# The first context tile in four chunks on a second queue, and the four denominator products issued together, in a cross-attention and mixture-of-experts kernel

## The chip, the cores and the metric

The kernel runs on one core of a Trainium2 chip. A core has a matrix engine (TensorE, PE in the profile, with its weight loads in a row of their own, PEld), a vector engine (VectorE, DVE), an activation engine (ScalarE, ACT), a general engine (GpSimd, POOL) and a sync engine (SyncE, SP) that issues most of the transfers. Each engine runs its own instructions in order and waits on semaphores for the others. The metric is the device time of the one core in microseconds. Three runs of the kernel before took 637.48, 638.38 and 639.96 us; their median is 638.38 us.

## The reference

The inputs are a batch of four sequences x of 512 tokens, width 512, and a context of 1,024 rows for each. The computation is one block of cross-attention and one feed-forward layer with eight experts, each behind a layer norm and added to x. The attention is the linear kind, in 16 heads of width 32:

```python
q = feature_map(norm(x) @ Wq.T)             # feature_map: x > 0 ? x + 1 : exp(x)
gate = sigmoid(norm(x) @ Wg.T + bg)
k, v = split(ctx @ Wkv.T)                   # feature_map on k
kv_summary = einsum('bhsd,bhse->bhde', k, v)
z = 1.0 / (einsum('bhld,bhd->bhl', q, k.sum(-2))[..., None] + EPS)
attn = einsum('bhld,bhde->bhle', q, kv_summary) * z
x = x + (attn * gate) @ Wo.T
```

Then every token of the new x goes to the two experts (of eight) with the largest logits, and their outputs are added with softmax weights.

## The kernel before

Everything is float32. A product is one `matmul` call of at most 128 x 128 weights against 512 columns; in the trace each such call stands as two matmul records[...].

**Setup.** SP issues all input transfers in the order of the program (`load`, L92). The first is `ctx_tiles[0, 0] = load_ctx(0, 0)` (L118): one 256 KB transfer of the first 128 context rows, already transposed in memory, so that each partition gets one row of 2,048 B, which holds four chunks `c` of 128 columns. Then come the four chunks of the key half of `wkv` (L121, 256 KB each), the second context tile, the four chunks of the value half, and the rest. The first matmul of the program, `pk` for tile (0, 0), multiplies chunk 0 of the context tile with chunk 0 of `wkv`, and so needs the first two transfers; the next needs the next chunk of `wkv`, and so on.

**Context.** For each batch `kv_tiles` (L281) goes over eight tiles of 128 context rows. A tile takes four products for its keys (`pk`), the feature map on DVE and ACT (L200 to L202), four products for its values (`pv`), which ACT copies out of PSUM (L258), and four small products that add the tile before to the sums (`kvs`).

**Queries.** For each batch the main loop (L692) makes `pq` (16 products), `pg` for the gates (16, with a sigmoid on ACT that writes `aT`, L325), the denominators `pd` (4 products with 32 output columns each) and their inverse `z` on DVE (L340, L341). Then it calls `products` (L344, called at L720).

**Products.** `z` holds one row for each head. `pz[g]` spreads these rows over the 128 partitions of group `g` by a product with a constant 0/1 matrix: 32 rows of the array, all 128 columns, at row offset `32 * g`. `pn[g]` are the numerators: for each group four products of 32 rows and 32 columns, each in its own place of the array. DVE multiplies `aT` by `pz` (L373) and by `pn` (L374). The groups go in two pairs, and PE gets its instructions in the order of the program (`keep_in_program_order`, L86): two `pz`, eight `pn`, two `pz`, eight `pn`.

What follows depends on the batch. For batches 0 to 2, the first half of the next batch's context tiles comes next (L723), so that PE goes on with `pk` and `pv` of the next batch's tile 0. For batch 3 it is the first four tiles of the experts' work (L725): each takes four transposes (`pt`), a copy on ACT, and four products (`pe`). Only after that does `attention_out` (L727) use `aT`.

**Buffers.** All these PSUM tiles come from one pool of six buffers (`pmm`, tag `mm`, L76), used in turn: a product may start when the reader of the tile that is six places ahead in this order is done.

**The second half** routes tokens to experts. Rows are scattered to a stream in device memory by indirect transfers, read back as tiles of 128 rows, multiplied with the expert's weights (`pe`, 35 tiles), scattered to `result`, and read back and added to `x` at the end.

Of the kernel before, what the change touches and what calls it, by code (L numbers as in the profile page):

```python
# [9 lines left out]
F32 = mybir.dt.float32  # L10
# [3 lines left out]
ALU = mybir.AluOpType  # L14
# [3 lines left out]
P = 128  # L18
B, L, S, D = 4, 512, 1024, 512
E, F = 8, 512  # L20
HD = 32
NC = D // P
NT = L // P
NS = S // P
# [7 lines left out]
ROW = D + 2  # L32
# [16 lines left out]
def xattn_moe_kernel(  # L49
# [14 lines left out]
    nc = tc.nc  # L64
# [6 lines left out]
    cpool = ctx.enter_context(tc.tile_pool(name="ctx", bufs=3))  # L71
# [4 lines left out]
    pmm = ctx.enter_context(tc.tile_pool(name="pmm", bufs=6, space=PSUM))  # L76
# [8 lines left out]
    def matmul(**operands):  # L85
        tc.keep_in_program_order(nc.tensor.matmul(**operands))  # L86
# [5 lines left out]
    def load(dst, src):  # L92
        tc.keep_in_program_order(nc.sync.dma_start(out=dst, in_=src))

    def load_ctx(b, s):
        t = cpool.tile([P, ROW], F32, tag="cT", name=f"cT_{b}_{s}")
        t = t[:, 0:D].rearrange("p (c n) -> p c n", n=P)
        load(t, cT[b, s])
        return t
# [15 lines left out]
    we_sb = wpool.tile([P, E, NC, F], F32, name="we_sb")  # L115

    ctx_tiles = {}
    ctx_tiles[0, 0] = load_ctx(0, 0)  # L118
    for half in range(2):
        for c in range(NC):  # L120
            load(wkv_sb[:, c, ts(half, D)], wkv[:, c, ts(half, D)])  # L121
        if half == 0:
            ctx_tiles[0, 1] = load_ctx(0, 1)
# [35 lines left out]
    spread = const.tile([P, NC, HD], F32, name="spread")  # L159
    nc.gpsimd.memset(spread, 1.0)  # L160
    for g in range(NC):
        r = slice(g * HD, (g + 1) * HD)
        for i in range(NC):
            o = (i + g) % NC
            nc.gpsimd.affine_select(
                out=spread[r, o, :], in_=spread[r, o, :], pattern=[[0, HD]],
# [8 lines left out]
        out=before, in_=before, pattern=[[1, P]], compare_op=ALU.is_gt, fill=0.0,  # L175
# [21 lines left out]
    def feature_map(dst, src):  # L197

        ex = work.tile([P, D], F32, tag="ex", name="ex")
        nc.vector.tensor_scalar(ex, src, 0.0, None, ALU.min)  # L200
        nc.scalar.activation(ex, ex, AF.Exp)  # L201
        nc.vector.scalar_tensor_tensor(dst, src, 0.0, ex, ALU.max, ALU.add)  # L202
# [34 lines left out]
    def half_tile(ct, half, name):  # L237
        ps = pmm.tile([P, D], F32, tag="mm", name=name)
        for c in range(NC):
            matmul(  # L240
                out=ps,
                lhsT=ct[:, c, :],
                rhs=wkv_sb[:, c, ts(half, D)],
                start=(c == 0),
                stop=(c == NC - 1),
            )
        return ps

    def keys(b, s):
        k = kvpool.tile([P, D], F32, tag="k", name=f"k_{b}_{s}")  # L250
        feature_map(k, half_tile(ctx_tiles[b, s], 0, "pk"))
        return k

    def values(b, s):
        pv = half_tile(ctx_tiles.pop((b, s)), 1, "pv")
        v = kvpool.tile([P, NC, P + 1], F32, tag="v", name=f"v_{b}_{s}", bufs=2)
        nc.gpsimd.memset(v[:, :, P : P + 1], 1.0)  # L257
        nc.scalar.copy(v[:, :, 0:P], pv.rearrange("p (g f) -> p g f", f=P))  # L258
        return v

    def kv_add(psum, s, k, v):

        for g in range(NC):
            matmul(
                out=psum[:, g, 0 : P + 1],
                lhsT=k[:, ts(g, P)],
                rhs=v[:, g, :],
                start=(s == 0 and g % 2 == 0),
                stop=(s == NS - 1),
                skip_group_check=True,  # L270
            )
# [6 lines left out]

    sums, pending, made = {}, {}, {}

    def kv_tiles(b, lo, hi, between=None):  # L281
        for s in range(lo, hi):
            nxt = (b, s + 2) if s + 2 < NS else (b + 1, s + 2 - NS)
            if nxt[0] < B and nxt != (0, 2):
                ctx_tiles[nxt] = load_ctx(*nxt)
            if b in (1, 2) and s % 2 == 0:
                e = (b - 1) * E // 2 + s // 2
                load(we_sb[:, e], we[e])
            if (b, s) == (3, 0):
                load(stream[SLOTS : SLOTS + P, :], empty)  # L290
            if s == 0:
                sums[b] = pkv.tile([P, NC, 2 * P], F32, tag="kvs", name="kvs")
            k = made.pop(s) if s in made else keys(b, s)
            if (b, s) == (0, 0):
                made[1] = keys(0, 1)
            v = values(b, s)
            if s > 0:
                kv_add(sums[b], s - 1, *pending[b])
            pending[b] = k, v
            if between is not None:  # L300
                between(s - lo)
        if hi == NS:
            kv_add(sums[b], NS - 1, *pending[b])
# [14 lines left out]
    def query(g, xT):  # L318
        qT = work.tile([P, L], F32, tag="qT", name="qT", bufs=NC)
        feature_map(qT, project(wq_sb, g, xT, "pq"))  # L320
        return qT
# [21 lines left out]

    def products(qTs, z, aT):  # L344

        for groups in ((0, 1), (2, 3)):
            pz = {g: pmm.tile([P, L], F32, tag="mm", name="pz") for g in groups}
            pn = {g: pmm.tile([P, L], F32, tag="mm", name="pn") for g in groups}
            for g in groups:
                r = slice(g * HD, (g + 1) * HD)  # L350
                matmul(
                    out=pz[g],
                    lhsT=spread[r].rearrange("p o e -> p (o e)"),
                    rhs=z[r, :],
                    start=True,
                    stop=True,
                    tile_position=(g * HD, 0),
                )

            for i in range(NC):  # L360
                for g in groups:
                    r = slice(i * HD, (i + 1) * HD)
                    o = (i + g) % NC * HD
                    matmul(
                        out=pn[g][o : o + HD, :],
                        lhsT=h_kv[r, g, :],
                        rhs=qTs[g][r, :],
                        start=True,
                        stop=True,
                        tile_position=(i * HD, o),  # L370
                    )
            for g in groups:
                nc.vector.tensor_tensor(aT[:, g, :], pz[g], aT[:, g, :], ALU.mult)  # L373
                nc.vector.tensor_tensor(aT[:, g, :], pn[g], aT[:, g, :], ALU.mult)  # L374

    def attention_out(b, aT):
        for t in range(NT):
# [148 lines left out]
    def per_expert(name):  # L526
        return const.tile([P, E], F32, name=name)
# [164 lines left out]
    for b in range(B):  # L692
        more = b + 1 < B
        qTs = [query(g, xT) for g in range(2)]
        if b > 0:
            dispatch(b - 1)
        qTs += [query(g, xT) for g in range(2, NC)]
        aT = big.tile([P, NC, L], F32, tag="aT", name="aT")
        gate(0, xT, aT)
        z = inverses(qTs)  # L700
        for g in range(1, NC):
            gate(g, xT, aT)
        if not more:
            whole = per_expert("whole")
            nc.vector.tensor_scalar(whole, counts[b - 1], float(1 - P), None, ALU.add)
            full = tiles_of(whole, "full")
            held = [tiles_of(counts[1], "held2"), tiles_of(counts[2], "held3")]
            none = per_expert("none")
            nc.vector.memset(none, 0.0)
            ahead = per_expert("ahead")  # L710
            nc.vector.tensor_tensor(ahead, held[0], full, ALU.min)
            early_groups = spans([none, ahead, full], "A")
            early_list = listed(early_groups, EARLY, "A")
            be_sb = wpool.tile([P, E, F], F32, tag="wkv", name="be_sb")
            load(
                be_sb.rearrange("p e f -> p (e f)"),
                be.rearrange("(o e) f -> o (e f)", o=1).to_broadcast([P, E * F]),
            )
            early = run(early_list, 0, EARLY, True)
        products(qTs, z, aT)  # L720
        if more:
            xs[b + 1] = load_x(b + 1)
            kv_tiles(b + 1, 0, NS // 2)  # L723
        else:
            for _ in range(4):  # L725
                next(early)
        attention_out(b, aT)  # L727
        choice = choose(b, *layernorm_stats(xs[b]))
        if more:
            ln = layernorm_stats(xs[b + 1])  # L730
            xT = new_xT()

            def between(i):
                normalized_T(xT, i, xs[b + 1], *ln)
                next(choice)

            kv_tiles(b + 1, NS // 2, NS, between)
            next(choice)
            kv_blocks(sums[b + 1])
# [14 lines left out]
    _, many, upto = early_groups  # L754
# [59 lines left out]
    first, last = 2 * NT, (B - 1) * NT  # L814
# [76 lines left out]
```

## Time and profile before

The profiled execution took 640.01 us, of which the span from first to last instruction is 638.3 us; 1.7 us lie around it.

| engine | busy us | share of the span |
|---|---|---|
| PE (matmul) | 606.4 | 95% |
| PEld (weight load) | 301.6 | 47% |
| DVE | 236.1 | 37% |
| ACT | 135.5 | 21% |
| POOL | 109.0 | 17% |

The parts of the kernel that the change touches, from the page and the timeline:

| what | count | busy us | mean ns of one record |
|---|---|---|---|
| `pk` products | 256 records | 118.6 | 608 |
| `pg` products | 128 records | 56.7 | 595 |
| gate times `pz` on DVE, one | 16 | | 681 (median) |
| `pz` products | 32 records | | 640 (median) |
| `pn` products | 128 records | | 600 (median) |
| wait of PE before the first `pk` | 1 | 4.6 (idle) | |

A matmul record's own duration is not what it costs: matmuls are pipelined, and the next starts before the one before has ended. The cost of a step on PE is the distance between starts, which the timeline shows. In a line of the timeline the first number is the start in us from the span's start, the second the time until the group's last end, and `x8` the number of records in the group; the bracket gives the idle time before it and what ended that.

### The profile page before, as it was taken

Reading aid. Unit: us, or ns where it says so; the run is one execution under the profiler, and the core shown is the slowest. Engines: PE = TensorE matmul, PEld = TensorE weight load, DVE = VectorE, ACT = ScalarE, POOL = GpSimd, SP = SyncE. Lnnn points to the kernel's source line nnn. Section 1 sums busy time; section 2 is a strip of 40 time slices with the busy share of each in tenths; the row PEclk is TensorE's granted clock in tenths of the full one; section 3 lists DMA queues with packets and bytes.
Section 4 is the critical chain, followed back from the end, with each engine's and each line's share of the span. In section 5 each row is a group of like instructions: output and inputs, shape, how many; then the busy total and the mean of one; then the engine's idle time right before and its main releaser. Section 6 shows DMA issues by size and latency. Waiting matters only on the chain. (4 is left out here: it accounts for less than half of the span.)

```text
span 638.3 us, 6238 instructions
## 1 busy us (share of the span) xinstructions
PE 606.4 (95%) x2044; PEld 301.6 (47%) x2044; DVE 236.1 (37%) x562; ACT 135.5 (21%) x215; POOL 109.0 (17%) x244
## 2 busy tenths in 40 slices
PE   7999999999999999999999999999999999999950
PEld 3555543544564345455543544654444654444420
DVE  2222243126224521632534135148424272111583
ACT  1322222113322122042221113322111221111100
POOL 3100000000004000000230000005241354643420
PEclk9999999999999999999999999999999999999985
DMA  8611400220253023022130100033430269647768
GB/s 301 194 34 37 144 0 2 104 93 17 82 166 115 18 62 111 26 91 93 47 117 17 34 16 16 1 131 134 116 116 33 84 203 264 193 133 258 278 236 300
DMA packets 27376, 70.50 MB, mean 110 GB/s; under 512 B 4240, under 2 KB 4240, under 8 KB 25936
## 3 DMA queue, kind: packets, MB, share of 16 engines
q1 hardware_dynamic: 19680, 48.31, 23.7%
q0 software_dynamic: 5360, 17.60, 7.6%
q10 hardware_dynamic: 2304, 4.20, 1.8%
q8 instruction: 17, 0.28, 0.2%
q14 instruction: 15, 0.12, 0.1%
HBM read 45.93 MB, written 24.16 MB: 110 GB/s over the span
## 5 line engine op out<-in xcount | busy, mean ns | idle before, releaser
L86 PE MATMUL pe<-we_sb,xgT 128*128 x280 | 125.9, 594 | 1.1 <-issue 0.6
L86 PE MATMUL pk<-wkv_sb,cT 128*128 128x512 f32 x256 | 118.6, 608 | 4.6 <-DMA wkv_sb<-in_wkv_dram 4.6
L86 PE MATMUL pv<-wkv_sb,cT 128*128 128x512 f32 x256 | 114.9, 592 | 0.0
L86 PEld LDWEIGHTS pv<-wkv_sb,cT 128*128 128x128 f32 x256 | 48.6, 190 | 61.2 <-issue 61.0
L200 DVE TENSOR_SCALAR ex<-pk 128x512 f32<-128x512 f32 x32 | 22.0, 689 | 148.0 <-PE pk L86 148.0
L86 PEld LDWEIGHTS pe<-we_sb,xgT 128*128 128x128 f32 x280 | 50.6, 190 | 53.0 <-issue 52.0
L86 PEld LDWEIGHTS pk<-wkv_sb,cT 128*128 128x128 f32 x256 | 47.7, 194 | 58.1 <-issue 54.3
L257 POOL MEMSET v<- 128x4 f32 x32 | 3.3, 106 | 347.1 <-PE kvs L86 284.1
L201 ACT ACTIVATE ex<-ex 128x512 f32<-128x512 f32 x48 | 30.2, 630 | 138.7 <-DVE ex L200 128.8
L86 PE MATMUL pg<-xT,wg_sb 128*128 128x512 f32 x128 | 56.7, 595 | 0.0
L86 PE MATMUL pq<-xT,wq_sb 128*128 128x512 f32 x128 | 56.6, 596 | 0.0
L659 DVE TENSOR_TENSOR y<-pe,be_sb 128x512 f32<-128x512 f32 x35 | 24.1, 690 | 87.4 <-PE pe L86 73.5
L86 PE MATMUL po<-wo_sb,aT 128*128 128x512 f32 x128 | 55.6, 592 | 0.0
L225 ACT COPY xgT<-pt 128x512 f32<-128x512 f32 x35 | 20.3, 587 | 121.9 <-PE pt L89 103.5
L670 POOL DMA_INDIRECT result<-y,to x35 | 37.5, 1071 | 39.0 <-DVE y L659 32.1
L505 POOL DMA_INDIRECT stream<-row,slot x32 | 32.1, 1003 | 49.6 <-DVE cmp L533 22.5
L86 PEld LDWEIGHTS kvs<-v,k 128*128 128x128 f32 x256 | 33.3, 191 | 13.4 <-issue 13.4
L86 PEld LDWEIGHTS pg<-xT,wg_sb 128*128 128x128 f32 x128 | 24.0, 190 | 32.1 <-issue 32.1
L86 PEld LDWEIGHTS po<-wo_sb,aT 128*128 128x128 f32 x128 | 24.1, 190 | 29.2 <-issue 28.9
L86 PEld LDWEIGHTS pq<-xT,wq_sb 128*128 128x128 f32 x128 | 23.8, 190 | 27.3 <-issue 27.3
L86 PE MATMUL kvs<-v,k 128*128 128x129 f32 x256 | 34.0, 275 | 0.0
L202 DVE SCALAR_TENSOR_TENSOR k<-pk,ex 128x512 f32<-128x512 f32 x32 | 22.1, 691 | 24.1 <-ACT ex L201 24.0
(151 smaller groups left out, 445.6 us busy)
## 6 DMA issues: line engine op xcount, KB each, us to landing
xg<-stream SPq DMA_DIRECT2D x35, 257.0 KB
cT<-in_cT_dram SPq DMA_DIRECT2D x32, 256.0 KB
we_sb<-in_we_dram SPq DMA_DIRECT2D x8, 1024.0 KB
y<-result SPq DMA_DIRECT2D x16, 512.0 KB
x<-in_x_dram SPq DMA_DIRECT2D x16, 256.0 KB
out_dram<-x ACTq DMA_DIRECT2D x16, 256.0 KB
stream<-empty SPq DMA_DIRECT2D x9, 257.0 KB
wkv_sb<-in_wkv_dram SPq DMA_DIRECT2D x8, 256.0 KB
```

What stands on the lines that cost most here:

```text
L86: tc.keep_in_program_order(nc.tensor.matmul(**operands))
L200: nc.vector.tensor_scalar(ex, src, 0.0, None, ALU.min)
L201: nc.scalar.activation(ex, ex, AF.Exp)
L202: nc.vector.scalar_tensor_tensor(dst, src, 0.0, ex, ALU.max, ALU.add)
L225: nc.scalar.copy(dst, pt)
L257: nc.gpsimd.memset(v[:, :, P : P + 1], 1.0)
L505: put = nc.gpsimd.indirect_dma_start(out=stream, out_offset=bass.IndirectOffsetOnAxis(ap=slots[i][:, t, :], axis=0), in_=rows[t], in_offse ...
L659: nc.vector.tensor_tensor(y, pe, be_sb[:, ds(no, 1), :].rearrange("p o f -> p (o f)"), ALU.add)
L670: put = nc.gpsimd.indirect_dma_start(out=result, out_offset=bass.IndirectOffsetOnAxis(ap=home_i, axis=0), in_=y, in_offset=None,)
```

## The change

The first context tile is not loaded by `load_ctx` any more. Its four chunks are four transfers of their own, of 64 KB each (512 B to a partition), issued by ACT's queue; SP's queue begins with the first chunk of `wkv`.

In `products` the four `pz` are issued one after the other, ahead of all `pn`, and take four of the six buffers at once. DVE multiplies all four groups of `aT` by `pz` first. `products` becomes a generator that stops after each pair of groups: the second pair's eight `pn` and their two multiplications are now issued inside the next batch's first context tile, between its four `pk` and its four `pv` (batches 0 to 2), or after the first of the four expert tiles (batch 3). The load of the next batch's x is issued between the two halves, in the same place of SP's order.

```diff
-    ctx_tiles[0, 0] = load_ctx(0, 0)
+
+    first = cpool.tile([P, ROW], F32, tag="cT", name="cT_0_0")
+    ctx_tiles[0, 0] = first[:, 0:D].rearrange("p (c n) -> p c n", n=P)
     for half in range(2):
         for c in range(NC):
+            if half == 0:
+                tc.keep_in_program_order(
+                    nc.scalar.dma_start(out=ctx_tiles[0, 0][:, c, :], in_=cT[0, 0, :, c, :])
+                )
             load(wkv_sb[:, c, ts(half, D)], wkv[:, c, ts(half, D)])
...
-    def kv_tiles(b, lo, hi, between=None):
+    def kv_tiles(b, lo, hi, between=None, inside=None):
...
             if (b, s) == (0, 0):
                 made[1] = keys(0, 1)
+            if inside is not None and s == lo:
+                inside()
             v = values(b, s)
...
     def products(qTs, z, aT):

+        pz = [pmm.tile([P, L], F32, tag="mm", name="pz") for _ in range(NC)]
+        for g in range(NC):
+            r = slice(g * HD, (g + 1) * HD)
+            matmul(
+                out=pz[g],
+                lhsT=spread[r].rearrange("p o e -> p (o e)"),
+                rhs=z[r, :],
+                start=True,
+                stop=True,
+                tile_position=(g * HD, 0),
+            )
         for groups in ((0, 1), (2, 3)):
-            pz = {g: pmm.tile([P, L], F32, tag="mm", name="pz") for g in groups}
             pn = {g: pmm.tile([P, L], F32, tag="mm", name="pn") for g in groups}
-            for g in groups:
-                r = slice(g * HD, (g + 1) * HD)
-                matmul(
-                    out=pz[g],
-                    lhsT=spread[r].rearrange("p o e -> p (o e)"),
-                    rhs=z[r, :],
-                    start=True,
-                    stop=True,
-                    tile_position=(g * HD, 0),
-                )
...
+            if groups[0] == 0:
+                for g in range(NC):
+                    nc.vector.tensor_tensor(aT[:, g, :], pz[g], aT[:, g, :], ALU.mult)
             for g in groups:
-                nc.vector.tensor_tensor(aT[:, g, :], pz[g], aT[:, g, :], ALU.mult)
                 nc.vector.tensor_tensor(aT[:, g, :], pn[g], aT[:, g, :], ALU.mult)
+            yield
...
-        products(qTs, z, aT)
+        product = products(qTs, z, aT)
+        next(product)
         if more:
             xs[b + 1] = load_x(b + 1)
-            kv_tiles(b + 1, 0, NS // 2)
+            kv_tiles(b + 1, 0, NS // 2, inside=lambda: next(product))
         else:
-            for _ in range(4):
+            next(early)
+            next(product)
+            for _ in range(3):
                 next(early)
```

## The prediction, made before the changed kernel ran

> **What bounds the kernel now.** I read the page's busy times first, then the chain of waits, then what PE itself waits for, and last the timeline at the two places that the change touches.
>
> ```profile
> span 638.3 us, 6238 instructions
> PE 606.4 (95%) x2044; PEld 301.6 (47%) x2044; DVE 236.1 (37%) x562; ACT 135.5 (21%) x215; POOL 109.0 (17%) x244
> ...
> PE   7999999999999999999999999999999999999950
> ```
>
> From the chain of waits (start, length, what):
>
> ```profile
> 453.47 1.06 PE pz L86 x4
> 454.52 1.02 PE pn L86 x16
> 455.54 1.06 PE pz L86 x4
> 456.60 1.02 PE pn L86 x16
> ```
>
> From the list of waits of PE (total us, times, longest):
>
> ```profile
> PE pk L86 <- DMA wkv_sb<-in_wkv_dram: 4.6, 1, 4.6
> ```
>
> PE is busy in all slices but the first and the last two. In the chain, the products of batch 3 lie on the path that sets the end. PE's list of waits begins with one of 4.6 us, before its first matmul; the next is 2.8 us in three pieces. So PE time taken out of the middle comes off the end as long as no new wait fills it, and so does an earlier first matmul. The tail (PE's last matmul starts about 604; reading back, adding and storing follow) hangs on PE and moves with it.
>
> **The four spreading products.** Batch 0 in the timeline:
>
> ```profile
> 99.69 0.59 PE L86 MATMUL pg<-xT,wg_sb 128*128 128x512 f32 x1
> 100.22 1.13 PE L86 MATMUL pz<-z,spread 32*128 32x512 f32 x4
> 100.32 0.69 ACT L325 ACTIVATE aT<-pg,bg_sb 128x512 f32<-128x512 f32 x1 [2.75 <-PE pg L86]
> 101.27 1.09 PE L86 MATMUL pn<-qT,h_kv 32*32 32x512 f32 x16
> 101.54 1.29 DVE L373 TENSOR_TENSOR aT<-pz,aT 128x512 f32<-128x512 f32 x2 [7.53 <-PE pz L86]
> 102.29 1.13 PE L86 MATMUL pz<-z,spread 32*128 32x512 f32 x4
> ...
> 103.35 1.09 PE L86 MATMUL pn<-qT,h_kv 32*32 32x512 f32 x16
> ...
> 104.37 3.70 PE L86 MATMUL pk<-wkv_sb,cT 128*128 128x512 f32 x8
> ...
> 107.90 3.60 PE L86 MATMUL pv<-wkv_sb,cT 128*128 128x512 f32 x8
> ```
>
> Distances of starts: a `pz` pair 1.05, eight `pn` 1.02, a pair 1.06, eight `pn` 1.02, four `pk` 3.53. The two products of a pair start 7 ns apart in the trace's records, and the pair takes hardly more than one product would (two passes); they run beside each other, in different rows of the array. Four in four different row groups should do the same: 1.05 plus two more issues of 7 ns in the last pass, 1.07. That removes one pair, 1.06.
>
> It is not all gain. Where PE goes from one shape to another, a pass takes longer: the last full `pg` pass before `pz` is 0.53 instead of 0.43, and the four `pk` behind `pn` take 3.53 where the next four full products take 3.43 (starts 107.90 and 111.34 in the trace). So a change of shape costs 0.10 on each side of a full product. Before, the order full-pz-pn-pz-pn-full has five changes; after, it is full-pz-pn-pk-pn-pv, also five, but the new pair of changes is of the dear kind: 0.09 where `pk` ends and 0.10 where `pv` begins. From the first `pz` to the end of `pv`: before 4.15 + 3.53 + 3.43 = 11.11; after 1.07 + 1.02 + 3.53 + 0.09 + 1.02 + 3.53 = 10.26. **Gain 0.85 a batch.** In batch 3 the second `pn` group stands between `pe` and `pt`; I take 0.85 there too. Four batches: **3.4 us.**
>
> New waits, one by one. (a) The second `pn` tile now takes the buffer of the last gate, whose sigmoid ends at 100.32 + 0.69 = 101.01; it is wanted at 101.29. Covered by 0.28. (b) `pk` now takes the buffer of the first `pz`, free when DVE's first multiplication ends: 101.54 + 0.69 = 102.23. It is wanted at 100.22 + 1.07 + 1.02 = 102.31. Covered by under 0.1, the thinnest cover; without it everything behind `pk` on PE waits, up to 0.1 a batch, and I count nothing. (c) The second `pn` pair takes buffers that DVE frees by 103.5; wanted at 105.9. (d) DVE gets four multiplications by `pz` at 0.61 apart (to 104.1), two by `pn` (to 105.3), the minimum on `pk` (about 106.0), then the second two, ahead of L202. In the trace L202 waits 2.03 us for ACT, which loads a table (1.28) and takes the exponential (0.63); the two multiplications lie in that gap. (e) Batch 3: the first expert tile's rows have landed by 452.96 (POOL reads them then), the second's by 454.26, and the transposes are wanted at 453.40 + 2.09 = 455.5. The second transpose's buffer is free about 0.1 after it is wanted, inside the wait for ACT's copy that is there anyway (458.24 to 458.88). The four x loads stand in SP's order where they stood; no queue is reordered behind them. `aT` is wanted only at 134.5.
>
> **The start.** The timeline:
>
> ```profile
> 0.81 1.28 ACT L201 ACT_TABLE_LOAD   x1 [0.81 <-PEq L876]
> 0.82 0.41 SPq L93 DMA_DIRECT2D cT<-in_cT_dram  x1
> ...
> 1.28 1.84 SPq L93 DMA_DIRECT2D wkv_sb<-in_wkv_dram  x4
> ```
>
> and windows of one microsecond (busy time and records of PE, PEld, DVE, ACT, POOL; clock; DMA):
>
> ```profile
> 8.00:9.00 1.00, 1.00 (x2) 0.34 (x1) 0.00 (x0) 0.00 (x0) 0.00 (x0) 1.00 1.07 361
> 11.00:12.00 1.00, 1.00 (x4) 0.52 (x3) 0.77 (x2) 0.13 (x1) 0.00 (x0) 1.00 1.07 406
> ```
>
> By the trace's packet records data flow from 1.87; the context tile (256 KB) has landed at 3.09, the first weight chunk at 4.17, and the first matmul starts 0.47 later, at 4.64. After the change the weight chunk goes first on SP and only 64 KB of the tile must be there. Alone it would land at 3.09, 1.08 earlier (upper end). Beside it go ACT's packets of 512 B: the records give 13 ns for 128 B and 84 ns for 2,048 B, so about 27 ns, and 8 of them on each of the 16 engines make 0.22 for one chunk. ACT issues a chunk every 0.43 or so, so between one and three chunks get in beside it: 3.3 to 3.75. Lower end: all four go first, then the bytes ahead of the first matmul are those of before, gain 0. I take one and a half chunks, **0.7 us.**
>
> The Trainium skill speaks against this part: "DMA: Bandwidth & Descriptors", section "Issuing engines are not separate DMA queues", says that transfers from several engines run on the same 16 engines and interleave, so that a second queue saves only the time of issuing. By that alone the part is worth nothing: issue is not what the first matmul waits for, since data of `wkv` flow only from 2.92, 1.2 after its issue ended. The sums would be 3.4 by the rule and 4.1 by the rows. I follow the rows, since the gain comes not from bandwidth but from 320 KB instead of 512 KB ahead of the first product.
>
> Does an earlier start shift all of PE? The two lines of windows show 2 records a us at 8 and 4 at 11, so PE runs at half pace first (the clock column does not show it); passes become 0.43 apart at about 10.5. "TensorE: Matmul & The Clock Gate", Part 1, says that the clock is raised after a busy window of about 3.4 us that is free-running. If the same window ends it, 0.7 us earlier at half pace is worth 0.35; if the start crosses a window's edge, 1.7 more. On average that is 0.7, which I keep; the spread goes into the range. PE wants the second weight chunk about 1.8 after the first matmul, at 5.8; before, it landed at 5.54 with at least as many bytes ahead. ACT's four issues push its table load to 2.5, and the first exponential is at 11.87. SP now has four early transfers of its own; its next waits for one to land, about 3.3 instead of 3.16, for a tile wanted after 10.
>
> **Sum.** 3.4 + 0.7 = 4.1. Against the profiled execution, 640.01 - 4.1 = 635.9. That execution lies 1.6 above the median of the runs, 638.38, and at their upper edge (639.96); the median after should be 638.38 - 4.1 = **634.3 us.** About 0.5%, 3.2 us, is what a measurement of this kernel can tell from no change.
>
> **Rivals.**
> 1. *Both parts work* (0.62): 634.3; own range 632.8 to 635.8.
> 2. *The first transfer is hidden anyway* (0.18): ACT's chunks crowd out the weight chunk, or the half pace takes the gain. 638.4 - 3.4 = 635.0. For it: all data pass the same 16 engines, full from 2 us on.
> 3. *The change does not do what it says* (0.12): four wide products go as two pairs, or `pk` waits on DVE (point b). Then 1.06 is not saved and the 0.19 of changes of shape is paid: 638.4 + 0.8 - 0.7 = 638.5; with half of it, 636.6.
> 4. *Slower* (0.08): no row shows four products that each write all 128 columns; `pd` writes 32 columns in each of four, `pn` 256 in all, a `pz` pair 256. If PSUM cannot take 512 at once, they go one by one: eight passes of 0.43 plus 0.1, 3.5 us, 2.5 more than counted. It decides from 1.92 a batch (1.07 + 0.85), where the gain is gone. Price: 4 x (2.5 - 0.85) - 0.7 = +5.9, 644.3. Against it: the pair is at 7 ns, and "TensorE: Matmul & The Clock Gate", Part 3, measures 3.07 times for four row tiles of 32 rows and 512 columns. By that, four products of 0.86 take 4 x 0.86 / 3.07 = 1.12; by the rows 1.07, which I keep: 0.2 us in four batches.
>
> **Numbers.** Range: from both parts plus the clock's luck (632.5) to above rival 2 with some wait on DVE (636.8); rival 3's worse half and rival 4 lie outside. Faster: most of 1, half of 2: 0.68. Same: the rest of 1 and 2, most of 3: 0.24. Slower: 0.08.
>
> **What would show it.** Four `pz` in one group of eight records, 1.07 from `pn`; `pk` about 2.09 after the first `pz`, with no idle time that ends at DVE; `pv` about 1.1 later behind `pk` than now; first matmul at 3.8 to 4.2. Wrong if the `pz` group takes over 1.9, if PE waits on `aT<-pz`, or if the first matmul still starts at 4.6.

## The result, and the profile after

The changed kernel takes 634.37 us (median of eight runs, 633.87 to 635.83) against 638.64 us for the kernel before in the same session (eight runs). The ratio is 0.9934, with a 95% interval from 0.9919 to 0.9949: 4.2 us less, between 3.3 and 5.2. A second measurement, in another session (run e10 below), gave 0.9950 (0.9936 to 0.9963), 3.2 us less, between 2.4 and 4.1.

The page of the changed kernel, and its list of what PE waits for:

```profile
span 632.1 us, 6250 instructions
...
PE 601.8 (95%) x2044; PEld 300.1 (47%) x2044; DVE 235.9 (37%) x562; ACT 135.5 (21%) x215; POOL 108.5 (17%) x244
```

```profile
PE pk L86 <- DMA wkv_sb<-in_wkv_dram: 4.1, 1, 4.1
PE pt L89 <- DVE xn L222: 2.8, 3, 1.0
PE pe L86 <- ACT xgT L231: 0.5, 2, 0.3
```

PE's share is the same 95%: the time left the engine that sets the end. The wait for the first weights fell from 4.6 to 4.1 us, and no wait on DVE's multiplications joined the list. The first matmuls in the timeline, before and after:

```profile
4.64 9.90 PE L86 MATMUL pk<-wkv_sb,cT 128*128 128x512 f32 x16 [4.64 <-DMA wkv_sb<-in_wkv_dram]
```

```profile
4.11 9.02 PE L86 MATMUL pk<-wkv_sb,cT 128*128 128x512 f32 x16 [4.11 <-DMA wkv_sb<-in_wkv_dram]
```

The timeline of batch 0 after the change (start, length, engine, what; the last column is what ended idle time):

```profile
98.80 1.14 PE L86 MATMUL pz<-z,spread 32*128 32x512 f32 x8
98.90 0.69 ACT L333 ACTIVATE aT<-pg,bg_sb 128x512 f32<-128x512 f32 x1 [2.75 <-PE pg L86]
99.87 1.09 PE L86 MATMUL pn<-qT,h_kv 32*32 32x512 f32 x16
100.12 2.49 DVE L382 TENSOR_TENSOR aT<-pz,aT 128x512 f32<-128x512 f32 x4 [7.53 <-PE pz L86]
100.89 3.70 PE L86 MATMUL pk<-wkv_sb,cT 128*128 128x512 f32 x8
102.52 1.28 DVE L384 TENSOR_TENSOR aT<-pn,aT 128x512 f32<-128x512 f32 x2
104.52 1.09 PE L86 MATMUL pn<-qT,h_kv 32*32 32x512 f32 x16
104.62 0.69 DVE L206 TENSOR_SCALAR ex<-pk 128x512 f32<-128x512 f32 x1 [0.82 <-PE pk L86]
105.53 3.70 PE L86 MATMUL pv<-wkv_sb,cT 128*128 128x512 f32 x8
...
109.07 3.60 PE L86 MATMUL pk<-wkv_sb,cT 128*128 128x512 f32 x8
```

The eight records of `pz` stand in one line and cost 99.87 - 98.80 = 1.07 us, as two products did before. From the first `pz` to the end of `pv` it is 109.07 - 98.80 = 10.27 us, against 11.12 before (100.22 to 111.34).

The two profiled executions differ by more than the medians: 640.01 against 633.87, 6.1 us. Matching the same steps on PE in both traces shows where. The first matmul is 0.54 earlier. The sixteenth record is 1.42 earlier, because the half pace with which PE begins (records 0.85 apart instead of 0.43) also ended sooner after the first matmul (3.85 us after it instead of 5.63). The queries of the next three batches start 2.26, 3.11 and 3.95 earlier, and batch 3's `attention_out` 4.84: steps of 0.84, 0.85, 0.84 and 0.89, the four calls of `products`. A further 0.83 comes off around the first of the late expert tiles, where PE's `pe` waited in the profile of before but not in this one, and 0.47 after the last matmul. That wait, of 0.5 us or more, stands in the profiles of e1 to e8, all from chips 7 and 11, and in none of e9 to e12, from chip 0; it goes with the chip or the session and not with the change, and its cause is not known. The half pace and the end vary from run to run (below); the steps of the products do not.

### The profile page after: what moved, and what is told of

Same layout as the page of the kernel before. It is cut to its first block, busy times and chain, and to the rows that moved or that the text cites. A ratio compares the mean times of both kernels' runs of the same rounds, so it can differ in the third digit from the quotient of the medians.

```text
span 632.1 us, 6250 instructions
## 1 busy us (share of the span) xinstructions
PE 601.8 (95%) x2044; PEld 300.1 (47%) x2044; DVE 235.9 (37%) x562; ACT 135.5 (21%) x215; POOL 108.5 (17%) x244
## 3 DMA queue, kind: packets, MB, share of 16 engines
q10 hardware_dynamic: 2880, 4.46, 1.9%
## 5 line engine op out<-in xcount | busy, mean ns | idle before, releaser
L264 ACT COPY v<-pv 128x512 f32<-128x512 f32 x32 | 18.7, 584 | 53.5 <-PE pv L86 53.5
```

## The experiments

**e1, the new start alone**, and **e2, the new products alone**, each on the kernel before. The edits are the two halves of the change's diff: e1 has

```diff
-    ctx_tiles[0, 0] = load_ctx(0, 0)
+    first = cpool.tile([P, ROW], F32, tag="cT", name="cT_0_0")
+    ctx_tiles[0, 0] = first[:, 0:D].rearrange("p (c n) -> p c n", n=P)
...
+            if half == 0:
+                tc.keep_in_program_order(
+                    nc.scalar.dma_start(out=ctx_tiles[0, 0][:, c, :], in_=cT[0, 0, :, c, :])
+                )
```

and e2 all the rest.

> The kernel before with the new start alone: the first context tile in four chunks on ACT's queue. If fewer bytes ahead of the first product are what counts, the first matmul starts at 4.0 to 4.2 us instead of 4.64 and the time falls by about 0.5 us, blurred by up to 0.9 either way by where the clock's window falls. If the first transfer is hidden anyway (the half pace at the start takes the gain), the time falls by under 0.3 us. The products keep two pairs, 1.06 each, in all four batches.

> The kernel before with the new products alone. The sum of the prediction: 0.85 us in each of four batches, 3.4 us less in all, with the first matmul at 4.6 as before. If the difference between the two traces came mostly from the start, the clock or the change from early to late expert tiles, it is under 2 us here. Read from the trace: starts of pq, batch by batch, each earlier by a further 0.85 than before.

Measured: e1 639.23 us against 639.06, ratio 1.0004 (0.9994 to 1.0014) over 20 and 23 runs. e2 635.39 us, ratio 0.9929 (0.9905 to 0.9953). In e2's trace the first `pz` of the four batches start at 100.20, 217.09, 333.97 and 450.85: 116.88 apart, where before they are 117.73 apart (100.22, 217.94, 335.67, 453.40): 0.84 a batch, as in the sum. So the products alone give a gain of this size. The start alone brings no gain that 20 runs show, although PE starts earlier in e1:

```profile
4.05 9.61 PE L86 MATMUL pk<-wkv_sb,cT 128*128 128x512 f32 x16 [4.05 <-DMA wkv_sb<-in_wkv_dram]
```

**e4 and e5, chunks or queue.** e4 keeps the second queue and drops the chunks; e5 keeps the chunks and drops the second queue.

```diff
# e4
-            if half == 0:
-                tc.keep_in_program_order(
-                    nc.scalar.dma_start(out=ctx_tiles[0, 0][:, c, :], in_=cT[0, 0, :, c, :])
-                )
+            if (half, c) == (0, 0):
+                tc.keep_in_program_order(nc.scalar.dma_start(out=ctx_tiles[0, 0], in_=cT[0, 0]))
# e5
-                    nc.scalar.dma_start(out=ctx_tiles[0, 0][:, c, :], in_=cT[0, 0, :, c, :])
+                    nc.sync.dma_start(out=ctx_tiles[0, 0][:, c, :], in_=cT[0, 0, :, c, :])
```

> The changed kernel with the first context tile as one transfer of 256 KB, still on ACT's queue beside the weights on SP's. If the second queue is what helps, the first matmul starts at about 4.1 us as after the change. If the bytes ahead of the first product are what counts, both transfers share the engines, 512 KB must move before either is complete, and it starts at about 4.6.

> The changed kernel with the four chunks on SP's own queue, each ahead of its weight chunk, and no second queue. If the bytes ahead of the first product are what counts, 64 KB and 256 KB on one queue do as well: first matmul at 4.0 to 4.2 us. If the second queue is what helps, 4.5 or later.

The first matmul of each, from the timelines of e4 and of e5:

```profile
4.96 9.41 PE L86 MATMUL pk<-wkv_sb,cT 128*128 128x512 f32 x16 [4.96 <-DMA wkv_sb<-in_wkv_dram]
```

```profile
4.29 9.60 PE L86 MATMUL pk<-wkv_sb,cT 128*128 128x512 f32 x16 [4.29 <-DMA wkv_sb<-in_wkv_dram]
```

A whole tile on its own queue is later than before (4.96 against 4.64): the two transfers share the engines and both end late (complete at 4.64 and 4.83 us by their semaphores, where before the tile was at 3.44 and the first weight chunk at 4.51). Chunks on one queue do as well as the slowest profile of the changed kernel (4.31, e10), though 4.29 is past the 4.0 to 4.2 expected. So it is the bytes ahead of the first product. What the second queue adds to the chunks is 0.1 to 0.2 at most: of the five profiles with the new start four lie at 4.05 to 4.16, but e4 and e5 are one profile each. In e5 a wait of 0.5 us for a later context tile appears as well, which gives the gain back. Single times, 635.53 and 636.37 us, cannot tell such differences.

**e3, without the split.** `yield` is taken out, so that the second `pn` group follows the first at once.

```diff
             for g in groups:
                 nc.vector.tensor_tensor(aT[:, g, :], pn[g], aT[:, g, :], ALU.mult)
-            yield
...
-        product = products(qTs, z, aT)
-        next(product)
+        products(qTs, z, aT)
...
```

> The changed kernel without the split: all four pz, then both groups of pn one behind the other, and only then the next context tile (or expert tile). The dear change of shape (0.19 us a batch) goes, but the fourth pn tile takes the buffer of the second pz, which DVE frees only 0.6 us after it is wanted. Expected: PE waits about 0.6 in front of the second pn group, 0.4 us a batch or 1.6 us in all slower than the changed kernel. If the split is of no use (no wait on DVE), it is 0.2 a batch or 0.8 us faster than the changed kernel.

e3 takes 636.50 us, ratio 0.9964 (0.9944 to 0.9983). Its timeline:

```profile
98.76 1.14 PE L86 MATMUL pz<-z,spread 32*128 32x512 f32 x8
...
99.83 2.68 PE L86 MATMUL pn<-qT,h_kv 32*32 32x512 f32 x32
100.09 2.48 DVE L382 TENSOR_TENSOR aT<-pz,aT 128x512 f32<-128x512 f32 x4 [7.53 <-PE pz L86]
102.45 3.70 PE L86 MATMUL pk<-wkv_sb,cT 128*128 128x512 f32 x8
```

The two groups take 102.45 - 99.83 = 2.62 instead of 2.04: 0.58 of waiting for the buffer that DVE's second multiplication frees, as expected. `pk` between the groups costs two dear changes of shape and covers this wait. By the starts of the next batches' queries e3 loses 0.37, 0.28 and 0.28 against the changed kernel, a little less than the 0.4 expected.

**e7, sixteen numerators at once.** In batches 0 to 2 the four groups' sixteen `pn` have sixteen different places in the array. With `pz` multiplied into `aT` while PE does `pk`, their four buffers are free.

```diff
+        if together:
+            spread_out()
+            yield
-        for groups in ((0, 1), (2, 3)):
+        for groups in ((0, 1, 2, 3),) if together else ((0, 1), (2, 3)):
...
-        product = products(qTs, z, aT)
+        product = products(qTs, z, aT, more)
```

(`spread_out` is the loop of four multiplications by `pz`.)

> The changed kernel with, in batches 0 to 2, the four pz, then the next tile's pk, then all sixteen pn in one group (sixteen different places of the array), then pv. If products in different places run beside each other however many they are, the sixteen pn take about 1.1 us as eight do, a batch saves 1.02 for one group, less nothing for changes of shape: 0.97 a batch, 2.9 us in all against the changed kernel. If PSUM or the issue limits them at eight, sixteen take 2.0, and the time stays within 0.3 us of the changed kernel.

631.96 us, ratio 0.9887 (0.9863 to 0.9910), against 0.9934 for the changed kernel. Its timeline:

```profile
98.76 1.14 PE L86 MATMUL pz<-z,spread 32*128 32x512 f32 x8
...
99.83 3.70 PE L86 MATMUL pk<-wkv_sb,cT 128*128 128x512 f32 x8
...
103.46 1.14 PE L86 MATMUL pn<-qT,h_kv 32*32 32x512 f32 x32
...
104.53 3.70 PE L86 MATMUL pv<-wkv_sb,cT 128*128 128x512 f32 x8
...
108.07 3.60 PE L86 MATMUL pk<-wkv_sb,cT 128*128 128x512 f32 x8
```

Sixteen `pn` cost 1.07, eight cost 1.02; from `pz` to the end of `pv` it is 9.31 instead of 10.27. The batches' first `pz` are 115.92 apart, another 0.97 less. Batch 3 keeps two groups, since its expert tiles take the buffers of the queries that `pn` still reads.

**e6 and e8, zeros on PE during the first transfers.** Added to the changed kernel (e6) and to e7 (e8):

```diff
+    warm = const.tile([P, P], F32, name="warm")
+    nc.vector.memset(warm, 0.0)
+    idle = pmm.tile([P, P], F32, tag="mm", name="idle")
+    for _ in range(6):
+        matmul(out=idle, lhsT=warm, rhs=warm, start=True, stop=True)
```

> The changed kernel with six products of a 128x128 tile of zeros by itself on PE while the first transfers are under way (1.3 to 4.1 us); nothing of the result uses them. If the half pace of the first matmuls is a clock that rises after a stretch of PE work, the full pace begins about 2.5 us earlier against the first real matmul, and the time falls by 1.0 to 1.5 us on average. If it has another cause (cold data, the transfers), or if zeros do not count as work, the first real matmuls stay 0.85 apart[...], and the time does not change or rises by up to 0.3.

> Both of the last two together: the sixteen pn in one group and the products of zeros at the start. If both hold, about 4 us less than the changed kernel, 630.3 us; if only the sixteen do, 631.5.

e6: 633.95 us, 0.9914 (0.9893 to 0.9935). e8: 631.56 us, 0.9887 (0.9862 to 0.9912), the lowest median of all, but not apart from e7. In e8:

```profile
1.13 2.93 PE L86 MATMUL idle<-warm 128*128 128x128 f32 x12 [1.13 <-DVE none L732]
4.46 7.32 PE L86 MATMUL pk<-wkv_sb,cT 128*128 128x512 f32 x16 [0.40 <-DMA wkv_sb<-in_wkv_dram]
```

The first sixteen records take 7.32 us instead of 9.02: by the trace's clock record the full pace begins at 4.91 in e8, 3.8 us after the first product of zeros and only 0.45 after the first real one. Without zeros it never came sooner than 3.1 after the first real one. So in e8 the zeros counted as work, and the half pace is a matter of the clock. e6 does not show it: there the full pace begins at 7.28, 3.0 after the first real matmul (4.26). Little of it reaches the time. PE now runs into the next limits, 0.4 us for the weights and 0.2 for a context tile in e8. Against e7, in the same session, e8's median is 0.4 less, inside the intervals, and its last matmul starts 0.76 earlier; 631.56 us is what was expected (631.5) if only the sixteen hold. For e6 there is no changed kernel in its session. Set against before in each session, it gains 0.8 us more than the changed kernel by the medians and 1.3 more by the ratios, with overlapping intervals, so whether the 1.0 to 1.5 us expected are there is not settled.

**e9 to e12, what the start is worth.** e9 puts the whole first tile behind the four weight chunks on SP; e10 is the changed kernel, e11 is e2, e12 is e7 with the start of before.

```diff
# e9, against the changed kernel
-            if half == 0:
-                tc.keep_in_program_order(
-                    nc.scalar.dma_start(out=ctx_tiles[0, 0][:, c, :], in_=cT[0, 0, :, c, :])
-                )
...
         if half == 0:
+            load(ctx_tiles[0, 0], cT[0, 0])
             ctx_tiles[0, 1] = load_ctx(0, 1)
```

> The changed kernel with the whole first context tile on SP behind the four weight chunks of the keys, so that the first matmul is late on purpose: about 7.4 us (the fifth transfer of before had landed at 6.93). If the first matmul's time passes to the end one for one, the time rises by 3.3 us against the changed kernel, to about 637.7. If only half of it passes (the clock's window is fixed, and half-pace time is worth half), 1.6. If the start is hidden by something else, it stays within 0.5 us.

> The changed kernel itself, for the difference to the next run on the same chip. If the start is worth what its first matmul shows, 0.5 us less than the products alone; if the start alone gives nothing, as it did without the new products, the same within 0.3.

> The new products with the start of before, for the difference to the run above. If the products carry all of the gain, the ratio to before is the same as the changed kernel's, 0.993; if 0.5 us belong to the start, it is 0.0008 higher, 0.9942 for 3.7 us less.

> The sixteen pn in one group with the start of before: a second pair with and without the new start. If the start is worth 0.5 us, 632.5; if it is hidden, 632.0, as with it.

| run | median us | ratio to before (95%) | first matmul us | 16th record us |
|---|---|---|---|---|
| e9, tile last | 639.07 (22 runs) | 1.0017 (1.0007 to 1.0027) | 8.96 | 17.41 |
| e10, changed | 634.53 (5) | 0.9950 (0.9936 to 0.9963) | 4.31 | 12.72 |
| e11, products alone | 635.55 (6) | 0.9960 (0.9946 to 0.9973) | 4.61 | 13.55 |
| e12, sixteen, old start | 632.02 (4) | 0.9906 (0.9891 to 0.9921) | 4.70 | 13.72 |

e9's first matmul is later than the 7.4 I had expected, so its rise is held against what it measured: 4.65 later than in e10, 4.70 later at the last matmul, and 4.54 more in the time. A start that is late by microseconds passes to the end one for one, and "hidden" is wrong as a rule.

At half a microsecond the answers differ. Four pairs of kernels differ in the start alone. With each median set against before in its own session, the new start is worth -0.2 us (e1 against before), 0.6 (changed against e2), 1.0 (e10 against e11) and 0.9 (e7 against e12); by the ratios it is -0.3, -0.3, 0.6 and 1.2, and no pair's intervals lie apart. The medians of e7 and e12 are nearly equal (631.96 and 632.02), but e12 ran on chip 0, where before also took 0.86 less than on e7's chip (638.20 against 639.06). e11, at 0.9960, lies above both values expected for it, and e10 above the first measurement of the same kernel. The clock blurs all of them, and so does the end, as DVE's list of waits from 595 us on shows, first in the profile of before, then in e1's:

```profile
DVE x L803 <- DMA y<-result: 7.3, 4, 5.7
DVE x L803 <- SPq L835: 2.2, 1, 2.2
```

```profile
DVE x L808 <- DMA y<-result: 6.8, 4, 5.7
DVE x L808 <- SPq L840: 4.4, 2, 3.2
```

L835 (L840 in e1) is the condition around the last expert tiles. DVE, which adds and evicts in order, waits there for 1.9 to 2.4 us in ten profiles, and for 3.7 to 4.5 in four (e1, e2, e9, e11). In e1 the last matmul starts 0.93 earlier than before, and the span is 0.9 longer: the time from the last matmul to the end is 25.55 us instead of 23.70.

## Why the prediction was right, point by point

**The forecast** was 634.3 us, 4.1 less, and 634.37 was measured, 4.2 less by the ratio. That the two agree to 0.1 us is partly luck, since one of its two terms is not shown in the time, and the second measurement gave only 3.2.

**The four products: right, by mechanism and size.** 0.85 a batch was worked out; 0.84, 0.85 and 0.84 were measured, and 0.89 in batch 3. The group of four takes 1.07, as derived from the pair's 1.05 and 7 ns an issue. The path from `pz` to the end of `pv` was put at 10.26 and is 10.27, with the dear changes of shape where the sum had them. (What the prediction calls a pass is one of the two records of a product.) The kernel with this gain alone gave 0.9929 as e2 and 0.9960 as e11, 4.5 and 2.6 us, and the 3.4 of the sum lies between; the times bear out its sign and rough size, the starts in the trace its exact size.

**The new waits: right.** `pk` starts at 100.89, 2.09 after the first `pz`, with DVE's first multiplication over at 100.81; the thin cover held. The last gate's sigmoid ends at 99.59, before `pn` at 99.87. DVE's second pair of `pn` multiplications, at 105.69, lies inside ACT's table load. In batch 3 the wait of the first `pe` for ACT's copy stays.

**The start: the term that was mis-sized.** The prediction took 0.7 us for "one and a half chunks". Over the five profiles with the new start the first matmul is at 4.05 to 4.31, mean 4.15; over the four with the old one, 4.46 to 4.70, mean 4.60. So it is 0.45, or 0.39 if e6 and e8 are counted, whose first real matmul waits for the same weights (4.26 and 4.46). The estimate of 27 ns for a 512 B packet was exact (median 27 in the trace); the first weight chunk landed at 3.65, within 3.3 to 3.75, though later than the value taken. What the 0.45 does to the time is not shown: e1's interval allows a gain of at most 0.4 us, and e10 against e11 gives 1.0. That the bytes ahead of the first product and not the second queue are the cause is what e4 and e5 show, with one profile each, and they bear out the Trainium skill's rule in "DMA: Bandwidth & Descriptors", "Issuing engines are not separate DMA queues": transfers on two queues share the engines, and e4, which changes the queue alone, is 0.3 later.

**What was misread.** The last matmul of before starts at 614.6 us and not at about 604, and the tail behind it does not simply move with PE: it takes 22.7 to 25.6 us in the fourteen profiles. Half of rival 3 is 636.4 and not 636.6, since half of 4.24 us is 2.1. Neither changed the forecast.

**The rivals.** Four wide products do run side by side; rivals 3 and 4 are out, and PSUM takes 512 columns at once (sixteen `pn` and four `pz` both take 1.07). Rival 2, a hidden start worth 635.0, is the one that e1 could not tell from the forecast; e9 shows that its mechanism is no general rule.

**Still open:** whether the new start is worth anything between nothing and 1 us, and why DVE waits at the condition for 2 us in some executions and 4 in others.

## What to carry to other kernels

Price a step on PE by the distance of starts, not by the records' durations, and count each change of shape between full and tiled products (0.1 us here): the sum then holds to hundredths of a microsecond. Products in different places of the array are worth gathering until their buffers run out, and a full product put between two groups pays for its changes of shape by covering the wait for the buffers. For an effect of half a microsecond in 600, look for it in the trace where it arises, ask separately whether the end is steady enough for the time to show it, and set each time against that of before on the same chip.

## What the runs showed of the hardware that was not expected

Products of zeros can raise PE's clock as real ones do (e8: full pace at 4.91 us, 0.45 after the first real matmul). In the new-start profiles the full pace came at 7.2 to 9.1 us, in the old-start ones at 9.5 to 10.4, 3.1 to 6.0 after the first matmul: an earlier start happened to gain 1.1 us by the sixteenth record (12.66 on average against 13.79), more than its own 0.45. Records are 0.853 apart at half pace and 0.429 at full, so a start that is 0.45 earlier is worth only 0.23 by the sixteenth record if the full pace comes when it did; the rest is the full pace, which came 1.9 us earlier on average. When it comes is not tied to the kernel's start: it began at 7.23, 7.96 and 9.10 us in e7, the changed kernel and e1, and the stretch at full clock lasted 600.75, 604.16 or 607.57 us in all fourteen traces, which is 176, 177 or 178 times 3.413, so the clock changed in steps of 3.41 us, and where in such a step a run begins is luck. The trace's own clock record has this change at 7.96 us in the changed kernel, while the page's clock row shows full clock from the first slice.
